# Joining score halves by an accumulating DMA in one slot of four, instead of on VectorE in one slot of five

## The chip, the core and the metric

The kernel runs on one core of a Trainium2 chip. The metric is the device time of one execution in microseconds. A core has five engines that run their own instruction queues: TensorE (PE, matrix products), VectorE (DVE), ScalarE (ACT), GpSimd (POOL) and SyncE (SP, which here only issues DMAs). They wait for each other through semaphores.

## The reference

The program is a stack of four graph layers on x of shape (64, 256, 128) with one 256 x 256 adjacency matrix. Layers 0 to 2 (a gated graph network of five steps, a Chebyshev layer and a plain graph convolution, each behind a layer norm and a relu, with a residual sum) make up, with the projections and outputs of layer 3, about a fifth of PE's busy time. The other four fifths are the scores of layer 3, an attention layer with a score for every pair of nodes:

```python
s1 = jnp.einsum('bkf,ef->bke', x, W1)
s2 = jnp.einsum('bkf,ef->bke', x, W2)
pre = s1[:, :, None, :] + s2[:, None, :, :] + b_lin
h = jnp.where(pre >= 0, pre, ALPHA * pre)
e = jnp.einsum('bije,e->bij', h, a) + bias
attn = jax.nn.softmax(e, axis=2)
out = jax.nn.sigmoid(jnp.einsum('bij,bjf->bif', attn, x))
```

For each of 64 batches and each of 256 x 256 pairs (i, j), 256 features e pass a leaky relu and are summed with weights a. The relu part is nonlinear in i and j together, so it has to be formed for every pair: 64 x 256 x 256 x 256 elements.

## The kernel before

Everything is float32. Two batches form a pair (NB = 2), so there are 32 pairs. The 256 features of a score are cut into two halves of 128, one feature to a partition: half 0 and half 1 (`k` in the code). The 256 rows i are cut into **slots**: a slot is four rows i, 32 apart, for both batches. A pair has 64 slots (two blocks `ic` of 32), the program 2048 (`NSLOT`).

A half of a slot is a tile `rl` of 128 partitions x (4 rows, 2 batches, 256 nodes j) = 128 x 2048 floats, 1 MiB. It holds min or relu terms of `s1[i] + s2[j]`, with the weights' sizes already folded into s1 and s2 (their signs are applied by the products on PE). PE then sums it over the features with four matmuls, side by side in four groups of 32 columns (`win` and `win_n` hold the signs and put the four rows at their place in the bank `pe`). Each float32 matmul shows as two records in the profile. There are 12 tiles `rl`.

A half-tile can be made by three engines:

- VectorE makes half 0 with one whole `tensor_tensor` of 128 x 2048 (L809).
- ACT makes half 1 with eight activations of 128 x 256 (L823).
- GpSimd makes either half with eight `tensor_scalar` of 128 x 256 (L835).

In one slot of five (`SHARE = (1, 5)`, 409 of 2048) the two halves are **joined** (`k == 2`): GpSimd makes a tile `z` of half 1 with a second form of row (L832, with the clamps `s1h` and `s1l`), and VectorE then adds half 0 into it with eight `scalar_tensor_tensor` (L801), which take the minimum and add what the tile holds. A joined tile goes to PE once instead of twice, so PE does 3687 half-tiles instead of 4096.

The order of each engine's instructions is fixed when the program is built. A small planner in the kernel keeps a clock for each engine (`clock`, advanced by `ran(engine, us, ...)` with durations written in the code), takes the engine whose time is least, and lets it do the first of what is ready: steps of a block's tail (softmax and output), then steps of a later pair's layers 0 to 2 (`front`), then score work. `in_order()` pins what was traced to that order. `part_of(e)` says which half an engine makes next, `tile_ready` when it could, `work_on_tile` does one part of it, `score` hands a finished tile to PE and returns it to `tiles` at the time when PE will have read it. `held` and `MOST` limit how many tiles each engine may have out. `partners` is the list of GpSimd's `z` tiles that wait for VectorE. The planned durations are, for example:

```python
done = ran(DVE, 1.55, since)      # four joining rows
done = ran(DVE, 2.2, since)       # a whole tile
done = ran(ACT, 1.43, since)      # four activations
done = ran(POOL, 1.06 if k == 2 else 0.9, since)   # two rows
```

Elsewhere in the pair's work GpSimd also does the subtraction of the gated step (L503), the inverse roots of the norms (L329, L330), a product of the norm (L402) and additions in the tail (L687, L725, L726), and VectorE waits for some of these.

Of the kernel before, what the change touches and what calls it, by code (L numbers as in the profile page):

```python
# [10 lines left out]
OP = mybir.AluOpType  # L11
# [4 lines left out]
NB = 2  # L16
# [4 lines left out]
MOST_NEGATIVE = -3.4028234663852886e38  # L21
PE, DVE, ACT, POOL = ENGINES = (mybir.EngineType.PE, mybir.EngineType.DVE, mybir.EngineType.Activation, mybir.EngineType.Pool)
SLOTS = 64
SHARE = (1, 5)
AHEAD_OF = 2


@with_exitstack
def kernel(
# [50 lines left out]
    nc = tc.nc  # L80
# [22 lines left out]
    def ran(engine, us, *after):  # L103
        start = max(clock[engine], 0.0, *after)
        if engine == ACT:
            behind[0] = max(0.0, behind[0] - (start - clock[ACT])) + 0.024 * us
        clock[engine] = start + us
        return clock[engine] + SEEN[engine] + (behind[0] if engine == ACT else 0.0)
# [19 lines left out]
    last, done = {}, [0]  # L128
# [208 lines left out]
    def flat(t):  # L337
        return t.rearrange("p b n -> p (b n)")
# [393 lines left out]
    NSLOT = NPAIR * SLOTS  # L732
    tiles = [[relu_pool.tile([P, 4, NB, N], F32, name=f"rl{k}", bufs=1), 0.0] for k in range(12)]
    MOST = {DVE: 8, ACT: 3, POOL: 4}
    held = dict.fromkeys(MOST, 0)
    begun = {}
    made = []
    partners = []
    left = {}
    t_pe = {}  # L740
    t_s2v = [0.0, 0.0]
    TAILED = set()
    ALONE, JOINED = [], []
    for n in range(NSLOT):
        (JOINED if (n + 1) * SHARE[0] // SHARE[1] > n * SHARE[0] // SHARE[1] else ALONE).append(n)
    following = [0, 0, 0]

    def where(n):
        return n // SLOTS, n % SLOTS // 32, n % 32

    def slot(k):

        of = JOINED if k == 2 else ALONE
        return of[following[k]] if following[k] < len(of) else NSLOT

    def part_of(e):

        if e == DVE:
            return 0
        if e == ACT:  # L760
            return 1
        if slot(2) <= max(slot(0), slot(1)) + AHEAD_OF:
            return 2
        return 0 if slot(0) < slot(1) else 1

    def tile_ready(e):

        if e in begun:
            return 0.0
        if e == DVE and partners and min(partners)[1] <= slot(0) + AHEAD_OF:  # L770
            return min(partners)[0]
        k = part_of(e)
        n = slot(k)
        if n >= NSLOT or n // SLOTS not in READY or held[e] == MOST[e] or not tiles:
            return None
        since = READY[n // SLOTS]["since"]
        return max(since[k], min(t[1] for t in tiles))

    def work_on_tile(e):
        if e not in begun:  # L780
            if e == DVE and partners and min(partners)[1] <= slot(0) + AHEAD_OF:
                since, n, t = partners.pop(partners.index(min(partners)))
                held[POOL] -= 1
                begun[e] = [n, 2, t, since, 0]
            else:
                k = part_of(e)
                tiles.sort(key=lambda t: t[1])
                begun[e] = [slot(k), k, *tiles.pop(0), 0]
                following[k] += 1
            held[e] += 1  # L790
        n, k, t, free, part = begun[e]
        p, ic, r = where(n)
        ops = READY[p]
        i0 = ic * P + r
        if e == DVE and k == 2:
            since = max(ops["since"][0], free)
            parts = 2
            for g in (2 * part, 2 * part + 1):
                for b in range(NB):
                    i = i0 + g * 32  # L800
                    nc.vector.scalar_tensor_tensor(t[:, g, b, :], ops["s2a"][:, b, :], ops["s1"][0][:, b, i:i + 1], t[:, g, b, :],  # L801
                                                   op0=OP.min, op1=OP.add)
            done = ran(DVE, 1.55, since)
            t_s2v[p % 2] = max(t_s2v[p % 2], done)
        elif e == DVE:
            since = max(ops["since"][k], free)
            whole = [P, 4, NB, N]
            rows = ops["s1"][0][:, :, i0:i0 + 97:32].rearrange("p b g -> p g b").unsqueeze(3)
            nc.vector.tensor_tensor(t, rows.to_broadcast(whole), ops["s2a"].unsqueeze(1).to_broadcast(whole), op=OP.min)  # L809
            done = ran(DVE, 2.2, since)  # L810
            t_s2v[p % 2] = max(t_s2v[p % 2], done)
            parts = 1
        elif e == ACT:
            since = max(ops["since"][k], free)
            if "s2p" not in ops:
                ops["s2p"] = s2p
                nc.scalar.copy(s2p, ops["s2n"])
                ran(ACT, COPY, since)
            parts = 2
            for g in (2 * part, 2 * part + 1):  # L820
                for b in range(NB):
                    i = i0 + g * 32
                    nc.scalar.activation(t[:, g, b, :], s2p[:, b, :], AF.Relu, bias=ops["s1"][1][:, b, i:i + 1], scale=-1.0)  # L823
            done = ran(ACT, 1.43, since)
        else:
            since = max(ops["since"][k], free)
            parts = 4
            for b in range(NB):
                i = i0 + part * 32
                row = slice(i, i + 1)  # L830
                if k == 2:
                    nc.gpsimd.tensor_scalar(t[:, part, b, :], ops["s2z"][:, b, :], ops["s1h"][:, b, row], ops["s1l"][:, b, row],  # L832
                                            op0=OP.min, op1=OP.max)
                else:
                    nc.gpsimd.tensor_scalar(t[:, part, b, :], ops["s2n" if k else "s2c"][:, b, :], ops["s1"][k][:, b, row],  # L835
                                            MOST_NEGATIVE, op0=OP.min, op1=OP.max)
            done = ran(POOL, 1.06 if k == 2 else 0.9, since)
        begun[e][4] += 1
        if part + 1 == parts:
            del begun[e]  # L840
            if e == POOL and k == 2:
                partners.append((done, n, t))
            else:
                made.append((done, n, k, t, e))

    def score_ready():

# [15 lines left out]
    def score(tile_):  # L863
        since, n, k, t, e = tile_
        p, ic, r = where(n)
        block = p * NC + ic
        pe = pes[block % 2]
        first = block not in left
        if first:
            left[block] = 64  # L870
        made.remove(tile_)
        left[block] -= 2 if k == 2 else 1

        w = win[:, 1] if e == ACT else win_n[:, k % 2]
        for g in range(4):
            nc.tensor.matmul(pe[g * 32:(g + 1) * 32, :], w[:, 31 - r:63 - r], flat(t[:, g]),  # L876
                             start=first, stop=(left[block] == 0), skip_group_check=True)
        free = ran(PE, PROJECT, since, t_pe.get(block - 2, 0.0))
        tiles.append([t, free])
        held[e] -= 1  # L880
        scored[0] += 2 if k == 2 else 1
        if left[block] == 0:
            begin((p, ic), tail(p, ic, pe, free, READY[p]["x3"], READY[p]["h3"]))
# [42 lines left out]
    while scored[0] < 2 * NSLOT or CHAINS:  # L926
        while begun_fronts[0] < NPAIR and begun_fronts[0] < 2 + (scored[0] + 2 * SLOTS - 1) // (2 * SLOTS):
            begin_front()
        e = min(now, key=now.get)
        todo = []  # L930
        for key in CHAINS:
            since = chain_ready(key, e)
            if since is not None:
                todo.append((since, (0, key) if isinstance(key, tuple) else (1, key), key))
        if e == PE:
            best = score_ready()
            if best:
                todo.append((best[0], (2,), best[1]))
        else:
            since = tile_ready(e)  # L940
            if since is not None:
                todo.append((since, (2,), None))
        ready = [x for x in todo if x[0] <= now[e] + 0.05]
        if ready:
            _, (rank, *_), what = min(ready, key=lambda x: x[1])
            if rank < 2:
                advance(what)
            elif e == PE:
                score(what)
            else:  # L950
                work_on_tile(e)
            in_order()
            now[e] = max(now[e], clock[e])
        else:
            later = [x[0] for x in todo] + [t for t in now.values() if t > now[e]]
            now[e] = min(later) if later else now[e] + 1.0
# [31 lines left out]
```

## Time and profile before

| | us |
|---|---|
| median of 3 runs | 5054.16 (5053.93 to 5054.52) |
| the profiled execution | 5031.67 |
| its span, first to last instruction | 5029.9 |
| idle of VectorE in the span | 199.3 |
| idle of ACT in the span | 230.8 |
| idle of GpSimd in the span | 195.7 |

Granted TensorE clock over the span: 0.996. The first 120 us are a ramp: the constants are prepared and the first pair goes through layers 0 to 2 before scores can start; GpSimd is busy 15.8 us of these 120. DMA is idle most of the time: 37.38 MB are moved in the whole span, 7 GB/s.

How to read it: busy time counts instructions as the profiler saw them, per engine and not counting DMA issues, branches or semaphore waits. A group's row gives the line and engine, what it writes and reads, the count, the busy time, the mean duration of one instruction in ns, and the idle time of the engine just before them with what ended it. Neighbouring instructions of one engine overlap, so a mean times a count can exceed the busy time. A row of the waits reads: who waited, for whom, microseconds in total, times, and the longest.

### The profile page before, as it was taken

How to read it: one execution, taken by the hardware profiler on the slowest of the kernel's cores; microseconds unless marked ns; L12 is line 12 of the kernel's file. 1: busy time of each engine (PE TensorE's matmuls, PEld its weight loads, DVE VectorE, ACT ScalarE, POOL GpSimd, SP SyncE). 2: the span in 40 equal slices, each digit the busy share in tenths (PEclk: the TensorE clock that was granted, in tenths of full speed). 3: DMA queues.
4: the chain of work that ended last, by engine and by line, in shares of the span. 5: the costliest groups of instructions: out<-in, count | busy, mean ns of one | idle time of the engine just before them, and what ended most of it. 6: DMA issues, size and time to landing. Idle time of an engine off the chain costs nothing.

```text
span 5029.9 us, 137362 instructions
## 1 busy us (share of the span) xinstructions
PE 4926.6 (98%) x52817; PEld 1791.9 (36%) x52817; DVE 4830.6 (96%) x6767; ACT 4799.1 (95%) x12553; POOL 4834.2 (96%) x9670
## 2 busy tenths in 40 slices
PE   7999999999999999999999999999999999999999
PEld 3333333333333333333333333333333333333332
DVE  3999999999999999999999999999999999999998
ACT  3999999999999999999999999999999999999999
POOL 1999999999999999999999999999999999999998
PEclk9999999999999999999999999999999999999999
DMA  0000000000000000000000000000000000000000
GB/s 20 8 7 6 9 5 9 9 5 8 7 7 9 6 7 8 8 6 8 6 8 8 6 9 6 8 8 5 9 8 5 9 8 6 8 5 6 6 5 4
DMA packets 60356, 37.38 MB, mean 7 GB/s; under 512 B 4528, under 2 KB 59696, under 8 KB 59696
## 3 DMA queue, kind: packets, MB, share of 16 engines
q1 hardware_dynamic: 58976, 28.59, 2.4%
q8 instruction: 413, 6.77, 0.6%
q14 instruction: 247, 2.02, 0.1%
q10 hardware_dynamic: 720, 0.00, 0.0%
HBM read 18.09 MB, written 10.49 MB: 6 GB/s over the span
## 4 chain that ended last, share of the span: by engine, by line
PE 43%; POOL 25%; DVE 23%; ACT 7%; issue 3%; DMA 0%; POOLq 0%; ACTq 0%; DVEq 0%
PE bank L876 26%; PE bank L335 14%; POOL rl L835 13%; DVE rl L809 12%; POOL rl L832 9%; ACT rl L823 6%; DVE rl L801 5%; POOL d L503 1%; PE bank L363 1%; DVE hT L510 1%; DVE bank L506 1%; DVE stats L395 1%; POOL mv L330 1%; PE bank L356 1%; POOL sc L687 0%
## 5 line engine op out<-in xcount | busy, mean ns | idle before, releaser
L823 ACT ACTIVATE rl<-bank,s1b 128x256 f32<-128x256 f32 x10536 | 4186.4, 908 | 9.2 <-PE bank L876 7.3
L809 DVE TENSOR_TENSOR rl<-s1a,bank 128x2048 f32<-128x2048 f32 x1269 | 2841.4, 2274 | 1.3 <-PE bank L876 1.2
L876 PE MATMUL bank<-rl,win_n 128*32 128x512 f32 x18960 | 2458.7, 595 | 26.7 <-DVE rl L809 19.4
L832 POOL TENSOR_SCALAR rl<-s2z,s1h,s1l 128x256 f32<-128x256 f32 x3272 | 1750.5, 551 | 0.0
L876 PE MATMUL bank<-rl,win 128*32 128x512 f32 x10536 | 1436.5, 594 | 0.0
L835 POOL TENSOR_SCALAR rl<-s2c,s1a 128x256 f32<-128x256 f32 x2960 | 1339.3, 474 | 14.0 <-ACT s1a L667 2.1
L801 DVE SCALAR_TENSOR_TENSOR rl<-bank,s1a,rl 128x256 f32<-128x256 f32 x3272 | 1324.7, 471 | 1.7
L835 POOL TENSOR_SCALAR rl<-s2n,s1b 128x256 f32<-128x256 f32 x2576 | 1167.7, 475 | 9.0
L876 PEld LDWEIGHTS bank<-rl,win_n 128*32 128x32 f32 x18960 | 629.5, 110 | 1339.8 <-issue 949.6
L876 PEld LDWEIGHTS bank<-rl,win 128*32 128x32 f32 x10536 | 356.1, 110 | 697.0 <-issue 567.0
L335 PE MATMUL bank<-mT,wts 128*32 128x512 f32 x2560 | 344.0, 593 | 1.2 <-DVE rh L468 1.2
L335 PE MATMUL bank<-adj_t,h 128*32 128x256 f32 x5120 | 315.3, 383 | 4.0 <-ACT h L522 3.8
L503 POOL TENSOR_TENSOR d<-d,hT 128x512 f32<-128x512 f32 x155 | 199.2, 1285 | 54.3 <-ACT d L499 54.3
L335 PEld LDWEIGHTS bank<-adj_t,h 128*32 128x32 f32 x5120 | 169.2, 111 | 166.2 <-issue 53.6
L406 ACT ACTIVATE h<-x,mv 128x128 f32<-128x128 f32 x384 | 168.2, 590 | 50.5 <-POOL mv L402 50.1
L412 ACT COPY mT<-bank 128x512 f32<-128x512 f32 x160 | 144.9, 906 | 42.9 <-PE bank L335 31.1
L506 DVE SCALAR_TENSOR_TENSOR bank<-bank,d 128x512 f32<-128x512 f32 x160 | 110.6, 692 | 72.2 <-POOL d L503 71.5
L464 ACT ACTIVATE bank<-bank,gate_b 128x512 f32<-128x512 f32 x160 | 160.2, 1001 | 16.9 <-PE bank L335 15.8
L335 PE MATMUL bank<-hT,wts 128*32 128x512 f32 x1280 | 175.2, 593 | 0.0
L335 PE MATMUL bank<-mT,w 128*32 128x512 f32 x1280 | 169.9, 593 | 0.0
L335 PE MATMUL bank<-rh,u5t 128*32 128x512 f32 x1280 | 169.8, 592 | 0.0
L487 ACT ACTIVATE bank<-bank,gate_b 128x512 f32<-128x512 f32 x160 | 153.6, 960 | 15.1 <-PE bank L335 15.0
(134 smaller groups left out, 3507.9 us busy)
## 6 DMA issues: line engine op xcount, KB each, us to landing
xin<-in_x_dram SPq DMA_DIRECT2D x64, 128.0 KB, 2.3
lin<-row SPq DMA_DIRECT2D x32, 256.0 KB, 7.7
out_dram<-o SPq DMA_DIRECT2D x64, 128.0 KB, 1.8
row<-quarter SPq DMA_DIRECT2D x32, 64.0 KB, 1.5
w_raw<-in_L_gnn_w_w_dram SPq DMA_DIRECT2D x3, 128.0 KB, 3.0
th_raw<-in_L_gnn_Theta_dram SPq DMA_DIRECT2D x1, 320.0 KB, 3.9
adj_n<-in_adj_dram SPq DMA_DIRECT2D x1, 256.0 KB, 3.2
w_raw<-in_L_gnn_u_w_dram SPq DMA_DIRECT2D x2, 64.0 KB, 2.9
```

The lines of the kernel that those rows point to most:

```text
L335: nc.tensor.matmul(o[g:g + 32], w[:, g:g + 32], t, start=start, stop=stop, skip_group_check=True)
L406: nc.scalar.activation(h[:, k, :], s[:, k, :], AF.Relu, bias=mv[:, k, 0:1], scale=mv[:, k, 1:2])
L464: nc.scalar.activation(r[0], pr[0], AF.Tanh, bias=br, scale=0.5)
L487: nc.scalar.activation(pr[0], pr[0], AF.Tanh, bias=bz, scale=0.5)
L503: nc.gpsimd.tensor_sub(d, d, hT)
L506: nc.vector.scalar_tensor_tensor(by_feature(pr[0]), by_feature(pr[0]), 1.0, d, op0=OP.add, op1=OP.mult)
L801: nc.vector.scalar_tensor_tensor(t[:, g, b, :], ops["s2a"][:, b, :], ops["s1"][0][:, b, i:i + 1], t[:, g, b, :], op0=OP.min, op1=OP.add)
L809: nc.vector.tensor_tensor(t, rows.to_broadcast(whole), ops["s2a"].unsqueeze(1).to_broadcast(whole), op=OP.min)
L823: nc.scalar.activation(t[:, g, b, :], s2p[:, b, :], AF.Relu, bias=ops["s1"][1][:, b, i:i + 1], scale=-1.0)
L832: nc.gpsimd.tensor_scalar(t[:, part, b, :], ops["s2z"][:, b, :], ops["s1h"][:, b, row], ops["s1l"][:, b, row], op0=OP.min, op1=OP.max)
L835: nc.gpsimd.tensor_scalar(t[:, part, b, :], ops["s2n" if k else "s2c"][:, b, :], ops["s1"][k][:, b, row], MOST_NEGATIVE, op0=OP.min, op1=O ...
L876: nc.tensor.matmul(pe[g * 32:(g + 1) * 32, :], w[:, 31 - r:63 - r], flat(t[:, g]), start=first, stop=(left[block] == 0), skip_group_check= ...
```

## The change

In a joined slot both halves are now made as ordinary tiles: half 0 by VectorE or GpSimd in their ordinary way, half 1 by GpSimd in the `z` form. When both are done, GpSimd issues one DMA that reads `z` and adds it into half 0's tile; PE takes the sum. The joining rows on VectorE are gone. The share goes from one slot in five to one in four (512 slots). In the planner, half 0's sequence now runs over all slots, half 1's over those that aren't joined, and `z` over the joined ones; an issue is planned at 0.7 us of GpSimd (`ISSUE`), a sum at 4.0 us of the DMA queue (`ADDED`) and 3.0 us more until it has landed (`LANDED`), and the issue is offered 0.3 us after the pair is done (`SLACK`), only between GpSimd's tiles. `z` is free when the sum has landed.

```diff
-SHARE = (1, 5)
+SHARE = (1, 4)
 AHEAD_OF = 2
+ISSUE, ADDED, LANDED, SLACK = 0.7, 4.0, 3.0, 0.3
...
-    partners = []
...
-    ALONE, JOINED = [], []
-    for n in range(NSLOT):
-        (JOINED if (n + 1) * SHARE[0] // SHARE[1] > n * SHARE[0] // SHARE[1] else ALONE).append(n)
+    JOINED = [n for n in range(NSLOT) if (n + 1) * SHARE[0] // SHARE[1] > n * SHARE[0] // SHARE[1]]
+    WITH = set(JOINED)
+    ORDER = [range(NSLOT), [n for n in range(NSLOT) if n not in WITH], JOINED]
     following = [0, 0, 0]
+    pairs = {}
+    adding = [0.0]
...
-        if e == DVE and k == 2:
-            since = max(ops["since"][0], free)
-            parts = 2
-            for g in (2 * part, 2 * part + 1):
-                for b in range(NB):
-                    i = i0 + g * 32
-                    nc.vector.scalar_tensor_tensor(t[:, g, b, :], ops["s2a"][:, b, :], ops["s1"][0][:, b, i:i + 1], t[:, g, b, :],
-                                                   op0=OP.min, op1=OP.add)
-            done = ran(DVE, 1.55, since)
-            t_s2v[p % 2] = max(t_s2v[p % 2], done)
-        elif e == DVE:
+        if e == DVE:
...
-            if e == POOL and k == 2:
-                partners.append((done, n, t))
+            if n in WITH:
+                pairs.setdefault(n, {})[k] = done, t, e
             else:
                 made.append((done, n, k, t, e))
+
+    def pair_ready():
+
+        return min(((max(x[0] for x in both.values()), n) for n, both in pairs.items() if len(both) == 2), default=None)
+
+    def add_pair(n):
+        (since, t, e), (since_z, z, e_z) = pairs[n][0], pairs.pop(n)[2]
+        nc.gpsimd.dma_start(out=t.rearrange("p g b n -> p (g b n)"), in_=z.rearrange("p g b n -> p (g b n)"), accum_op=OP.add)
+        issued = ran(POOL, ISSUE, since, since_z)
+        adding[0] = max(adding[0], issued) + ADDED
+        done = adding[0] + LANDED
+        held[e] -= 1
+        held[e_z] -= 1
+        tiles.append([z, done])
+        made.append((done, n, 2, t, None))
...
             if since is not None:
-                todo.append((since, (2,), None))
+                todo.append((since, (3,), None))
+            pair = pair_ready()
+            if e == POOL and pair and e not in begun:
+                todo.append((pair[0] + SLACK, (2,), pair[1]))
...
+            elif rank == 2:
+                add_pair(what)
             else:
                 work_on_tile(e)
```

## Prediction

> **What bounds the kernel now.** I read the busy table first, then the costliest groups, then the waits of GpSimd and VectorE, last the busy time by stretch and a piece of the timeline.
>
> ```profile
> span 5029.9 us, 137362 instructions
> PE 4926.6 (98%) x52817; PEld 1791.9 (36%) x52817; DVE 4830.6 (96%) x6767; ACT 4799.1 (95%) x12553; POOL 4834.2 (96%) x9670
> ```
>
> Four engines are full at once, so a gain has to lighten all four, or lighten the tightest by no more than its lead over the next. PE's figure is modelled at its ends: in the timeline the matmuls of consecutive half-tiles begin 0.86 us apart (2513.04, 2513.90, 2514.76), while a half-tile counts 1.06 us busy (3895.2 us of L876 over 3687 halves). So some 0.2 x 3687 = 740 us of PE's busy time on this line is overlap, and PE has slack that its 98% hides. PE follows; it doesn't lead.
>
> ```profile
> L823 ACT ACTIVATE rl<-bank,s1b 128x256 f32<-128x256 f32 x10536 | 4186.4, 908 | 9.2 <-PE bank L876 7.3
> L809 DVE TENSOR_TENSOR rl<-s1a,bank 128x2048 f32<-128x2048 f32 x1269 | 2841.4, 2274 | 1.3 <-PE bank L876 1.2
> L832 POOL TENSOR_SCALAR rl<-s2z,s1h,s1l 128x256 f32<-128x256 f32 x3272 | 1750.5, 551 | 0.0
> L835 POOL TENSOR_SCALAR rl<-s2c,s1a 128x256 f32<-128x256 f32 x2960 | 1339.3, 474 | 14.0 <-ACT s1a L667 2.1
> L801 DVE SCALAR_TENSOR_TENSOR rl<-bank,s1a,rl 128x256 f32<-128x256 f32 x3272 | 1324.7, 471 | 1.7
> L835 POOL TENSOR_SCALAR rl<-s2n,s1b 128x256 f32<-128x256 f32 x2576 | 1167.7, 475 | 9.0
> ```
>
> The producers of score halves are here, with almost no idle before them. Instructions of one engine overlap, so I divide busy time by count: ACT row 0.397 us, DVE whole tile 2.239, DVE joining row 0.405, GpSimd z row 0.535, GpSimd plain row 0.453 (2507.0 / 5536). Which engine is tightest shows in who waits:
>
> ```profile
> POOL d L503 <- ACT d L499: 54.3, 4, 16.1
> POOL mv L329 <- DVE mv L397: 34.8, 6, 17.0
> ...
> DVE bank L506 <- POOL d L503: 71.5, 62, 6.5
> ...
> DVE nmx L691 <- POOL sc L687: 15.3, 20, 2.1
> DVE x L598 <- POOL rn L330: 13.8, 16, 2.1
> ```
>
> GpSimd's two long waits fall into the ramp (10 waits, up to 17 us). From 200 to 4900 us it waits 1.0 us in all, while VectorE waits 83.3 us there on GpSimd (the last three rows, cut to that stretch: 55.6, 15.3 and 12.4). GpSimd is busy 4633 of those 4700 us, the rest being gaps between its own instructions; VectorE 4594, ACT 4555. **GpSimd leads**, by 39 us over VectorE and 78 over ACT. What the change puts on GpSimd decides.
>
> **What the Trainium skill says.** (1) "DMA: Bandwidth & Descriptors", section "Latency and other measured facts": a DMA issued by GpSimd takes about 1 us to its first byte, the time of the Q7 cores that write descriptors. The trace before has no DMA of GpSimd; SyncE's issue slices in the timeline are 0.34 and 0.36 us. (2) Same page, "Anatomy of one DMA — SWDGE (gpsimd) path": about 2.0 us plus bytes over 436 GB/s. "Collectives: The Full Stack", section "The bandwidth ceiling: the fold count and why AG ≠ RS ≠ AR", says that an add in the DMA reads two sources. No run here shows either; the largest transfer in the trace is 256 KB. (3) "SBUF — State Buffer", section "Who interferes with whom": DMAs don't contend with compute engines, and a VectorE instruction with one SBUF input doesn't contend with GpSimd. The trace agrees as far as it goes: the plain GpSimd rows have median 473 and minimum 458 ns, with VectorE at 96% beside them.
>
> **The change, part by part.** Counts come from the instruction orders of both kernels; each busy time is count by the durations above.
>
> VectorE loses 3272 joining rows (1324.7 us) and gains 571 whole tiles (1840 instead of 1269): 571 x 2.239 = 1278.5. Net -46 us.
>
> ACT loses 112 rows: 112 x 0.397 = -44 us.
>
> PE loses 412 matmuls, that is 103 of 3687 halves: 103 x 0.86 = -89 us. 409 joined slots become 512.
>
> GpSimd gains 824 z rows (4096 instead of 3272): +440.8. It loses 2008 plain rows (3528 instead of 5536): 2008 x 0.453 = -909.4. Net -468.6 before the 512 DMAs it now issues. **So an issue may cost 468.6 / 512 = 0.915 us before GpSimd is as loaded as today.**
>
> The issue is the unknown. Below: SyncE's 0.34 us, where GpSimd's own instruction would only start it. Above: 1.0 us by the skill's first-byte price, and up to 2.0 if two source reads double the descriptors. Nothing excludes values over 1.0. I take 0.7, the middle of 0.34 and 1.0; it is also what the kernel's own plan reserves (ISSUE), whose other GpSimd entries agree with the trace (0.9 for two plain rows against 0.906, 1.06 for two z rows against 1.07). GpSimd then stands at -468.6 + 358.4 = -110 us.
>
> The wait that the issue adds: GpSimd must see VectorE's half (and its own z) done, and its queue stands still behind it. In the new order at least one further GpSimd tile (8 rows, 3.6 to 4.3 us) lies between z's last row and the issue in 504 of 512 cases, and today GpSimd waits on VectorE 1 us in the steady stretch; I cost this at nothing, at worst some 0.1 us a time, 50 us, which the 110 us cover.
>
> The transfer: one tile is 1 MiB. Estimate from the page: 2.0 + 2 x 1.049 MB / 436 GB/s = 6.8 us; the plan allows 4.0 queued plus 3.0. One sum is due every 4970 / 512 = 9.7 us, so the DMA queue keeps up unless a sum takes over 9.7. SyncE's queue is untouched. Latency costs buffers, not time: holding times (making, some 2 us of waiting, 0.9 on PE; z 17 us and its partner 18 us, with 6 us of waiting and 7 of landing) add up to about 7 of the 12 tiles (36 ms of holding over 4970 us). Five spare tiles let a sum land about 5 x 4970 / 1024 = 24 us later than planned. PE's new wait for the sums I therefore cost at nothing.
>
> The sum: with GpSimd 110 us lighter, what is late next is VectorE or ACT. VectorE: 4784.4 busy and today's 199.3 us of idle is 4984; a third of the 83 us it waits on GpSimd may go, giving 4956. ACT: 4754.6 + 230.8 = 4985 with all its idle kept. I take a span of 4970, 60 us less. The profiled execution took 5031.67 us, 22.5 less than the median of the runs, 5054.16; I carry that over: 5054 - 60 = **4994 us**, -1.2%. (A measurement of this kernel tells about 0.2%, 10 us, from no change.)
>
> **The rivals.**
>
> *The issue becomes GpSimd's bound (slower).* One mechanism: the Q7 cores write descriptors for one target and two sources, and GpSimd's next row waits for them. It decides from 0.915 us; each 0.1 above adds 51 us, as GpSimd has no idle to give. At 1.0: 5054 + 44 = 5098; at 1.1: 5149; at 2.0: 5610. For it: the page's 1 us and GpSimd's lead. Against: first-byte time is latency[...]. From 0.80 down VectorE binds instead, and a cheaper issue gains nothing more.
>
> *The DMA is too slow (slower).* If an add in the DMA takes 12 us of the queue, 512 x 12 = 6144 us of span. Against it: 2.4 us of bytes per MiB, twice, leaves nearly half of the 9.7.
>
> *Gain eaten (same).* An issue of 0.9 to 0.93, or 0.8 plus 0.1 of waiting for VectorE's half each time: about 5054.
>
> *Not as said?* The order holds 512 DMAs and no joining row, so it does what it says; only the times are open.
>
> **How the numbers follow.** Issue under 0.89 and sums on time: 0.57. Level, 0.09. Issue above: 0.28. DMA late or rate-bound: 0.06. Likeliest: 4994, with its own range 4950 (all of VectorE's 83 us gone: 4784 + 116 = 4900, half believed) to 5040. To hold 8 in 10 it has to reach into the slower case up to an issue of 1.1: 5150. Left out: dearer issues and a slow DMA, some 0.15, and 0.03 below. Faster 0.57, same 0.09, slower 0.34.
>
> **What would show it.** In the profile after: no joining row on VectorE, 1840 whole tiles near 2.24 us; 512 issues on GpSimd's queue. Right: GpSimd's busy time near 4366 us (issues aren't counted), gaps of about 0.7 us around issues, VectorE's waits on GpSimd shorter, PE's waits on the DMA a few tens of us. Wrong by the first rival: gaps of 0.9 us or more at issues, VectorE's and PE's waits on GpSimd rows grown, GpSimd again without waits. Wrong by the second: PE or the rows that reuse a tile waiting on the DMA by hundreds of us.

## The result, and the profile after

The changed kernel took 5028.64 us (median of 4) against 5054.33 us before (4): ratio 0.9951, interval 0.9934 to 0.9968, a gain of 0.5%. Measured again beside other runs it took 5014.61 us (6 executions, 5005.26 to 5026.62) against 5029.99 (28): ratio 0.997 (0.9958 to 0.9981). Executions of the kernel before fall on two levels, near 5030 and near 5054, and no trace shows why. So below a variant is set against the changed kernel as it ran beside the same figure of before: 5028.6 where before has its median at 5054, and 5014.6 where it has it at 5030 (the runs again, with eleven tiles, and with both plan entries). Differences of 20 us across the two are not read.

The first table of the page after, to set beside that of before:

```profile
span 5030.7 us, 133280 instructions
PE 4827.5 (96%) x51993; PEld 1741.7 (35%) x51993; DVE 4806.1 (96%) x4066; ACT 4768.8 (95%) x12441; POOL 4754.5 (95%) x8998
```

Every engine has less to do: PE -99 us, VectorE -25, ACT -30, GpSimd -80. The profiled executions have the same span (5029.9 before), but they don't compare the kernels: that of before is 22 us faster than the other executions beside it, that of the changed kernel isn't. All four engines idle more: PE 203 us instead of 103, VectorE 225 instead of 199, ACT 262 instead of 231, GpSimd 276 instead of 196.

The costliest groups (busy us, mean ns; then idle time before the group's instructions, and what ended most of it); first PE's score line as it was before, then the page after:

```profile
L876 PE MATMUL bank<-rl,win_n 128*32 128x512 f32 x18960 | 2458.7, 595 | 26.7 <-DVE rl L809 19.4
...
L807 ACT ACTIVATE rl<-bank,s1b 128x256 f32<-128x256 f32 x10424 | 4147.6, 772 | 72.4 <-PE bank L875 54.0
L793 DVE TENSOR_TENSOR rl<-s1a,bank 128x2048 f32<-128x2048 f32 x1840 | 4098.0, 2277 | 90.2 <-DMA rl<-rl 43.6
L875 PE MATMUL bank<-rl,win_n 128*32 128x512 f32 x18248 | 2296.1, 597 | 108.9 <-DVE rl L793 70.6
L816 POOL TENSOR_SCALAR rl<-s2z,s1h,s1l 128x256 f32<-128x256 f32 x4096 | 2224.6, 620 | 16.7 <-PE bank L875 9.5
L819 POOL TENSOR_SCALAR rl<-s2n,s1b 128x256 f32<-128x256 f32 x1864 | 858.2, 517 | 23.9 <-PE bank L875 10.8
L819 POOL TENSOR_SCALAR rl<-s2c,s1a 128x256 f32<-128x256 f32 x1664 | 764.3, 516 | 12.8 <-DMA rl<-rl 0.4
L836 POOL DMA_DIRECT2D rl<-rl x512 | 414.3, 811 | 23.8 <-DVE rl L793 12.2
```

The counts are those of the orders: no joining row, 1840 whole tiles, 512 issues. What is new stands right of the second bar. VectorE's whole tiles had 1.3 us of idle before them; now 90.2. ACT's rows had 9.2; now 72.4. PE's `win_n` matmuls had 26.7; now 108.9. The issue is 414.3 / 512 = 0.81 us busy; unlike what stands above on how to read the page, GpSimd's busy time counts these issues.

The waits of VectorE, ACT and PE after (total us, times, longest):

```profile
DVE rl L793 <- DMA rl<-rl: 43.6, 30, 4.0
DVE rl L793 <- PE bank L875: 37.2, 45, 5.0
DVE bank L507 <- POOL d L504: 26.5, 23, 6.5
...
ACT rl L807 <- PE bank L875: 54.0, 41, 3.7
...
PE bank L875 <- DVE rl L793: 70.6, 75, 3.1
PE bank L364 <- DVE hT L511: 50.9, 52, 3.5
PE bank L875 <- DMA rl<-rl: 36.7, 30, 4.1
```

A row that makes a tile and waits for the DMA or for PE's score line waits for a **tile to come free**. Before, these waits on VectorE and ACT were 8.5 us; now they are 43.6 + 37.2 + 54.0 and 16.1 on ACT for the DMA: 151 us. VectorE's wait on GpSimd's L503 (71.5 before; L504 now) has shrunk to 26.5, as predicted.

The DMA queue of the sums and their landing, from the page after:

```profile
q0 software_dynamic: 73728, 536.90, 53.1%
...
rl<-rl POOLq DMA_DIRECT2D x512, 1024.0 KB, 7.5
```

The queue holds the engines for 0.531 x 5030.7 / 512 = 5.2 us a sum, where the plan says 4.0. A sum lands 7.5 us after its issue begins in the median (6.7 to 13.7); the plan says 0.7 + 4.0 + 3.0 = 7.7 for a sum that has the queue to itself. So a sum alone lands about when the order supposes. Those that queue behind another land later than supposed; in the trace 85 of the 512 issues start within 5.2 us of the one before.

### The profile page after: what moved, and what is told of

It reads as the page before. It is cut to its first block, busy times and chain, and to the rows that moved or that the text cites. A ratio compares the mean times of both kernels' runs of the same rounds, so it can differ in the third digit from the quotient of the medians.

```text
span 5030.7 us, 133280 instructions
## 1 busy us (share of the span) xinstructions
PE 4827.5 (96%) x51993; PEld 1741.7 (35%) x51993; DVE 4806.1 (96%) x4066; ACT 4768.8 (95%) x12441; POOL 4754.5 (95%) x8998
## 4 chain that ended last, share of the span: by engine, by line
PE 39%; DVE 27%; POOL 12%; DMA 7%; ACT 6%; issue 5%; POOLq 0%; DVEq 0%; ACTq 0%
PE bank L875 24%; DVE rl L793 21%; PE bank L336 13%; DMA rl<-rl 7%; POOL rl L816 5%; POOL rl L819 5%; ACT rl L807 4%; PE bank L364 1%; POOL rl L836 1%; DVE stats L396 1%; DVE hT L511 1%; DVE bank L507 1%; POOL d L504 1%; DVE rh L469 1%; PE bank L357 0%
## 5 line engine op out<-in xcount | busy, mean ns | idle before, releaser
L807 ACT ACTIVATE rl<-bank,s1b 128x256 f32<-128x256 f32 x10424 | 4147.6, 772 | 72.4 <-PE bank L875 54.0
L793 DVE TENSOR_TENSOR rl<-s1a,bank 128x2048 f32<-128x2048 f32 x1840 | 4098.0, 2277 | 90.2 <-DMA rl<-rl 43.6
L875 PE MATMUL bank<-rl,win_n 128*32 128x512 f32 x18248 | 2296.1, 597 | 108.9 <-DVE rl L793 70.6
L816 POOL TENSOR_SCALAR rl<-s2z,s1h,s1l 128x256 f32<-128x256 f32 x4096 | 2224.6, 620 | 16.7 <-PE bank L875 9.5
L875 PE MATMUL bank<-rl,win 128*32 128x512 f32 x10424 | 1382.0, 595 | 0.0
L819 POOL TENSOR_SCALAR rl<-s2n,s1b 128x256 f32<-128x256 f32 x1864 | 858.2, 517 | 23.9 <-PE bank L875 10.8
L819 POOL TENSOR_SCALAR rl<-s2c,s1a 128x256 f32<-128x256 f32 x1664 | 764.3, 516 | 12.8 <-DMA rl<-rl 0.4
L836 POOL DMA_DIRECT2D rl<-rl x512 | 414.3, 811 | 23.8 <-DVE rl L793 12.2
L504 POOL TENSOR_TENSOR d<-d,hT 128x512 f32<-128x512 f32 x155 | 214.1, 1381 | 60.5 <-ACT d L500 60.2
L465 ACT ACTIVATE bank<-bank,gate_b 128x512 f32<-128x512 f32 x160 | 147.9, 924 | 18.5 <-PE bank L336 17.4
L364 PE MATMUL bank<-ident,hT 128*128 128x128 f32 x640 | 105.6, 288 | 54.0 <-DVE hT L511 50.9
L336 PEld LDWEIGHTS bank<-mT,wts 128*32 128x32 f32 x2560 | 86.0, 111 | 192.5 <-issue 145.3
```

Source lines behind the costliest of these rows:

```text
L336: nc.tensor.matmul(o[g:g + 32], w[:, g:g + 32], t, start=start, stop=stop, skip_group_check=True)
L364: nc.tensor.transpose(pt[:, b, c, :], ht[:, b, c * P:(c + 1) * P], ident)
L465: nc.scalar.activation(r[0], pr[0], AF.Tanh, bias=br, scale=0.5)
L504: nc.gpsimd.tensor_sub(d, d, hT)
L836: nc.gpsimd.dma_start(out=t.rearrange("p g b n -> p (g b n)"), in_=z.rearrange("p g b n -> p (g b n)"), accum_op=OP.add)
```

## Experiments: what the sum costs

**No sums.** The order stays, the DMA goes; half 1 of the joined slots is left out of the scores.

```diff
-        nc.gpsimd.dma_start(out=t..., in_=z..., accum_op=OP.add)
```

> The changed kernel without the 512 sums: the plan and so the order of all other instructions is unchanged, but no DMA is issued and PE takes half 0's tile alone (half 1 of the joined slots is left out of the scores). Theory T (tiles: engines wait because z and its partner are held 7.5 us and more by a sum): all waits on the DMA and most on tile reuse go, and with them the issues' 414 us of GpSimd; time near 4960. Theory I (the issue on GpSimd costs the gain): the same near 4960, so this run gives only the sum of both. Theory P (PE and the dependences of layers 0 to 2 set the pace, VectorE's 25 us less is all there is): within 15 us of 5029.

4911.01 us, ratio 0.9729 (0.9705 to 0.9754), some 50 us below what the theories T and I expected. Theory P (the pace is set elsewhere) falls: against 5028.6 the sums cost the changed kernel 118 us in all. Its busy table:

```profile
PE 4784.2 (97%) x51993; PEld 1750.8 (36%) x51993; DVE 4775.6 (97%) x4066; ACT 4756.6 (97%) x12441; POOL 4396.2 (90%) x8486
```

Three engines are at 97%, GpSimd at 90% with room. The order is that of the changed kernel, so the difference of GpSimd's busy time is what the issues add to it: (4754.5 - 4396.2) / 512 = 0.70 us each. That is less than the 0.81 us of an issue's own record, because issues overlap the rows beside them.

**Short sums.** Each DMA carries 64 of 2048 columns; the other columns' sums are left out.

```diff
-...in_=z.rearrange("p g b n -> p (g b n)"), accum_op=OP.add)
+...in_=z.rearrange("p g b n -> p (g b n)")[:, 0:64], accum_op=OP.add)
```

(The destination is cut likewise.)

> The changed kernel with each sum cut to 64 of 2048 columns: the issue stays on GpSimd[...], the transfer shrinks to a thirty-second, order unchanged; the other columns' sums are left out. Theory T: as fast as the kernel without sums (near 4960), landing drops from 7.5 to about 2 us and the waits on the DMA (96 us on PE, VectorE, ACT) go. Theory I: as slow as the changed kernel, 5029, with an issue still near 0.81 us. Theory P: within 15 us of 5029 like the other.

4981.56 us (4969.56 to 4992.56), ratio 0.987 (0.9845 to 0.9895): between the theories. The executions form two groups, three near 4970 and three near 4992. The issue, the queue and the landing in its trace:

```profile
L836 POOL DMA_DIRECT2D rl<-rl x512 | 417.2, 817 | 15.1 <-DVE rl L793 8.6
...
q0 software_dynamic: 73728, 16.81, 4.1%
...
rl<-rl POOLq DMA_DIRECT2D x512, 32.0 KB, 2.2
```

The issue costs the same for 32 KB as for 1 MiB (0.815 and 0.809 us; the packets are as many, 144 a sum); landing falls from 7.5 to 2.2 us, and the waits on the DMA are gone (0.5 us left). So the **issue**, with what a short sum still takes, accounts for about 4982 - 4911 = 71 us, and the rest of the **transfer** for about 5029 - 4982 = 47 us. The two groups make each of these uncertain by 11 us.

## Experiments: the share

**VectorE's joining at one in four.**

```diff
-SHARE = (1, 5)
+SHARE = (1, 4)
```

(in the kernel before)

> The kernel before with its VectorE joining, but one slot in four joined: only the share moves. VectorE's joined slot costs 3.24 us against 2.24 for a half, GpSimd's z 4.28 against 3.62; PE has 103 halves less (-89 us). If the share alone brings PE's relief and PE sets the pace (P): up to 25 us faster than 5054. If VectorE and GpSimd set the pace: they get about 100 more joined slots, (103 x 1.0 us more on VectorE, 103 x 0.66 on GpSimd, 103 fewer halves of 3 to 4 us to make elsewhere): within 20 us of before, either way.

5124.45 us, ratio 1.0138 (1.0112 to 1.0164): my 20 us were wrong, it loses 71. By the expectation's prices the extra making is 103 x (1.0 + 0.66) = 171 us. Measured, the planner spreads somewhat more over three full engines: VectorE's busy time rises by 79 us (to 4909.8), ACT's by 83 (4881.7), GpSimd's by 67 (4901.3), while PE's 412 fewer matmuls buy nothing. Joining more slots is paid by the makers, not by one of them.

**The DMA's joining at one in five.**

```diff
-SHARE = (1, 4)
+SHARE = (1, 5)
```

(in the changed kernel)

> The changed kernel with one slot in five joined by a DMA (409 sums): the means of joining alone, at the share of before. 103 fewer issues and sums, 103 more halves on PE. T: fewer tiles held, fewer waits, but more making; between 5010 and 5035. P: PE back at 3687 halves, time 20 us or more over the changed kernel, near 5054.

5000.8 us (4989.16 to 5005.37), ratio 0.9905 (0.9884 to 0.9926): 28 us faster than one in four, and below the range of either theory. P falls again: PE had 103 halves more and the kernel was faster. The means of joining alone is worth more than the whole change; the larger share gave part of it back.

## Experiments: tiles and plan

**The changed kernel again.** No edit.

> The changed kernel again, unchanged, beside the others: executions of the kernel before fall on two levels, 5029.5 and 5053.7, and this tells on which levels the changed one falls. If the change brings the whole difference of the medians, 25 us, all its executions stay near 5028. If it has the same two levels, some come at about 5004.

5014.61 us, spread from 5005.26 to 5026.62: neither of the two cases expected.

**Eleven tiles** instead of twelve, in each kernel.

```diff
-... for k in range(12)]
+... for k in range(11)]
```

> The changed kernel with 11 tiles rl instead of 12 (the planner knows it and plans for it). Theory T (sums hold tiles and the 12 are too few): clearly slower, by 30 us or more over 5029, more waits of VectorE and ACT on PE's and the DMA's release of tiles. Theory P (pace set elsewhere, tiles to spare as the prediction said): within 10 us of 5029.

5093.82 us, ratio 1.0133 (1.0119 to 1.0146): 79 us lost.

> The kernel before with 11 tiles instead of 12. T: before, tiles are held shortly, so it loses little: within 10 us of 5054, less than a third of what the changed kernel loses by the same edit. P: the same loss in both.

5037.7 us, ratio 1.0015 (1.0008 to 1.0021): 8 us lost. The same edit costs the changed kernel ten times as much. GpSimd's largest wait in the changed kernel with 11 tiles:

```profile
POOL rl L816 <- DMA rl<-rl: 106.6, 22, 8.5
```

It waits for a tile that a sum still holds, 22 times and up to 8.5 us.

**Thirteen tiles**, with the ring of short-lived tiles cut from 12 to 9 buffers to make room.

```diff
-... for k in range(12)]
+... for k in range(13)]
...
-    SHORT = dict(tag="short", bufs=12)
+    SHORT = dict(tag="short", bufs=9)
```

> The changed kernel with 13 tiles rl; for their room the ring of short-lived tiles of layers 0 to 2 and the tails goes from 12 to 9 buffers, which may itself cost. With 11 tiles the changed kernel lost 79 us, the one before 8. If a tile more relieves the sums: 10 us or more under 5014. If the cut ring binds: above 5014, with new waits on layers 0 to 2, and it tells nothing on tiles.

5003.68 us, ratio 0.9899 (0.9887 to 0.9912): 25 us under 5028.6, with no run of the cut ring alone beside it. VectorE's waits for a tile fell from 80.8 to 18.1 us:

```profile
DVE rl L793 <- DMA rl<-rl: 10.8, 12, 2.8
DVE rl L793 <- PE bank L875: 7.3, 13, 1.4
...
PE bank L875 <- DMA rl<-rl: 33.5, 31, 3.8
```

PE's own wait for the sums stays (33.5 of 36.7). A tile more helps those who make tiles; it doesn't help PE, which is ordered to take some sums before they have landed. So tiles are a part, and the order is another.

**The plan's entries** raised: the queue's to what the trace shows, the issue's to 0.9, which lies above the 0.81 of its record and the 0.70 that it adds. Only the order of instructions and the division of halves change.

```diff
-ISSUE, ADDED, LANDED, SLACK = 0.7, 4.0, 3.0, 0.3
+ISSUE, ADDED, LANDED, SLACK = 0.9, 5.3, 3.0, 0.3
```

> The changed kernel with the plan's entries near what the trace shows (ISSUE 0.9 instead of 0.7: the issue is 0.81 us busy and about 0.1 us of gaps; ADDED 5.3 instead of 4.0: the queue is 53.1% busy, 5.2 us a sum; LANDED 3.0 kept). Only the order changes. If the misplanned order makes the waits on the DMA (96 us on PE, VectorE and ACT) they fall by half or more and the time drops to about 5005. If tiles are the cause, a later planned landing changes little: within 10 us of 5029.

4975.86 us (4973.78 to 4977.6), ratio 0.9892 (0.9879 to 0.9906) beside the 5029.99 of before: 39 us under the changed kernel in the same comparison, with the same 512 sums, the same issue (0.82 us) and the same landing (7.5 us). PE's waits in its trace:

```profile
PE bank L875 <- DVE rl L793: 89.0, 122, 3.1
PE bank L364 <- DVE hT L511: 29.4, 40, 2.4
PE bank L875 <- DMA rl<-rl: 6.7, 3, 5.0
```

Waits on the DMA are 6.7 us on PE, 1.4 on VectorE and 6.9 on ACT, 15 in all instead of 96, though the transfer is unchanged. What it still costs in this order isn't shown: no run has these entries with short sums. Which of the two entries did it:

```diff
+ISSUE, ADDED, LANDED, SLACK = 0.9, 4.0, 3.0, 0.3
```

> The changed kernel with only ISSUE planned at 0.9 us instead of 0.7 (ADDED stays 4.0): GpSimd gets fewer halves, the sums are still planned to land too early. Replanning both entries gave 4975.9 against 5014.6. If the late landing is the cause, this brings little: within 15 us of 5014. If GpSimd's overload by 0.11 us and more an issue (512 x 0.11 = 56 us) is the cause, this alone reaches 4985 or less.

4993.16 us (4987.0 to 4996.43), ratio 0.9877 (0.9864 to 0.989): 35 us under 5028.6, between the two cases expected. GpSimd makes 19 half-tiles fewer (152 rows), VectorE 10 and ACT 9 more. The waits on the DMA are only halved:

```profile
PE bank L875 <- DMA rl<-rl: 27.0, 24, 6.1
...
DVE bank L507 <- POOL d L504: 16.6, 6, 6.5
...
ACT h L407 <- POOL mv L403: 18.1, 20, 4.3
```

```diff
+ISSUE, ADDED, LANDED, SLACK = 0.7, 5.3, 3.0, 0.3
```

> The changed kernel with only ADDED planned at 5.3 us instead of 4.0 (ISSUE stays 0.7): sums are planned to land 1.3 us later, so PE and the reuse of tiles are ordered later. If the late landing is the cause: 4990 or less, and the waits on the DMA fall from 100 us to under 30. If GpSimd's overload is: within 15 us of 5014, the waits on the DMA fall all the same.

5022.15 us (5003.84 to 5026.48), ratio 0.9932 (0.9921 to 0.9943): 6 us under 5028.6. Its profiled execution, the fastest of the six, shows the waits on the DMA nearly gone (8.6 us on PE, 2.2 on VectorE, 6.9 on ACT). The waits on GpSimd are there instead, twice as long as with the issue's entry:

```profile
DVE bank L507 <- POOL d L504: 35.7, 23, 6.5
...
ACT h L407 <- POOL mv L403: 33.0, 32, 4.4
```

So most of the 39 us comes with the issue's entry, and waits on the DMA can go without the time following them. The two gains, 35 and 6, add up to about that of both; that one entry pays only with the other isn't shown. The likely reading is that with ISSUE at 0.7 the order gives GpSimd more than it does in time. Whether any other relief of GpSimd by some 19 half-tiles would do the same was not tried; the issue itself adds no more than the 0.7 that was planned.

**One in five with the new entries.**

```diff
-SHARE = (1, 4)
+SHARE = (1, 5)
...
+ISSUE, ADDED, LANDED, SLACK = 0.9, 5.3, 3.0, 0.3
```

> The changed kernel with both plan entries (0.9 and 5.3) and one slot in five joined (409 sums). With the old entries one in five was faster than one in four (5000.8). If that came only from the misplanned sums, one in four is now as fast or faster: here 4975 to 4995. If fewer sums are better in themselves: below 4970.

4977.7 us (4975.69 to 4980.53), ratio 0.9847 (0.9835 to 0.986): 23 us under one in five with the old entries. One in four with the new entries took 4975.86, but in the other comparison; so which share is better with them stays open. That the smaller share had won only because fewer of its sums were misplanned fits the expected range, and isn't shown. Both kernels beat the one before and the changed one.

## Why the prediction was right in direction and wrong in size

**Direction: right; mechanism: in part.** It is faster, by 26 us beside the figure of before that the forecast started from (15 in the second comparison), where 60 were forecast; the measured time lies inside the range of the likeliest case, 4950 to 5040. VectorE's and ACT's lighter load, GpSimd's shorter row list and VectorE's shorter waits on GpSimd are all in the trace. The next limit was not where the sum put it, at VectorE or ACT with the idle of today.

**The failed step: the waits costed at nothing.** "Latency costs buffers, not time", "about 7 of the 12 tiles", and "PE's new wait for the sums I therefore cost at nothing". Measured: waits for a tile on VectorE and ACT went from 8.5 to 151 us, PE waits 37 us for sums, and with the transfer cut to a thirty-second 47 us come back, more than the 34 that were missing. The occupancy was a mean, while sums can follow each other closely and then land up to 13.7 us after the issue; with one tile less the kernel loses 79 us, so there weren't five to spare. And the order is fixed at build time: it takes a sum from a queue that it advances by 4.0 instead of 5.2 us. I compared the queue's time with the 9.7 us between sums, which was right (the second rival didn't occur), but not with what the order supposes. The 6.8 us estimated for bytes and fixed cost against the planned 4.0 + 3.0 looked like agreement; they say nothing of how long a sum keeps the queue.

**The carried idle** is the same step seen in the sum. The floor of 4956 to 4985 kept the idle of VectorE and ACT, or took some off; in the profiles it grew by 25 and 31 us. Nor was it a floor: without the sums the kernel takes 4911, and VectorE and ACT idle 134 and 153 us there.

**The issue.** I took 0.7 us, and by the run without sums GpSimd's busy time grows by 0.70 an issue, under the 0.915 of the first rival. That rival did not occur: GpSimd waits more than before, it doesn't lead. But "a cheaper issue gains nothing more" was false: between short sums and none lie 71 us. And I read the plan's 0.7 as agreement, without asking what the order does with it; with 0.9 planned, 35 us come back. How 0.70 us on an engine that has room without them becomes that much isn't resolved.

**Two readings of the lines.** I added the busy times of groups that overlap each other. VectorE's whole tiles and joining rows are busy 4122 us together, not 2841.4 + 1324.7 = 4166, so its saving was 24 us and not 46. PE's two groups on the score line are busy 3447 us together, not 3895, so the slack hidden in its 98% is nearer 280 us than 740. The pitch of 0.86 us holds, though two of the three starts that I gave for it belong to L335. The largest transfer before was 320 KB, not 256.

**The offset.** The 22.5 us by which the median of before stood over its profiled execution is the distance between its two levels, 5030 and 5054. The changed kernel shows no such distance (profiled 5032.47, others 5028.3 to 5029.0). Carrying it did no harm only because before ran near 5054 again. It also makes the 10 us that I took for the least a measurement tells too fine.

**The prices used.** The 1 us of "DMA: Bandwidth & Descriptors", section "Latency and other measured facts", is a first-byte time and not how long GpSimd is held, which is 0.81 us here, and 0.70 net. The estimate from "Anatomy of one DMA — SWDGE (gpsimd) path" with the two sources of "Collectives: The Full Stack", section "The bandwidth ceiling: the fold count and why AG ≠ RS ≠ AR", 6.8 us, is close to the 7.5 us measured. Two sources fit the queue: 2 x 1.049 MB in 5.2 us are 403 GB/s of reading (a working from the trace; the reading itself isn't shown). The sentence on VectorE and GpSimd from "SBUF — State Buffer" holds there only outside VectorE's two-port modes, which the prediction left out. That DMAs don't slow the engines agrees with the traces: GpSimd's z rows have a median of 553 ns and VectorE's whole tiles one of 2277 or 2278 ns with the sums and without them.

**A rival not separated.** In the profiled execution of the changed kernel the granted TensorE clock dips more often than before (the figures are at the end). The mean is 0.992 instead of 0.996, at most some 20 us of PE's time; how much of it reaches the kernel's time was not tried.

## What to carry to other kernels

Where every engine is full and the order is fixed when the program is built, what an asynchronous step costs depends on what the plan supposes of it: here two planned durations were worth 39 us with the same transfers. Read issue, queue time and landing from the first trace, and try them in the plan before judging the step. A mean occupancy of buffers says little about spare ones; taking one buffer away, in both kernels, tells it in two runs. Groups of one engine overlap, so their busy times are not added: ask for the busy time of the instructions together. When a change carries two edits, such as the way of joining and its share, run each alone: here the way alone gained more than both.

## What the runs showed of the hardware

- The issue of an accumulating DMA on GpSimd is busy 0.81 us for 128 rows of 8 KB and 0.815 us for 128 rows of 256 bytes, with 144 packets a sum in both: at this number of rows it does not depend on the bytes. Landing does: 7.5 and 2.2 us.
- 512 such issues add 358 us to GpSimd's busy time in the same order, 0.70 us each.
- An accumulating DMA of 1 MiB from one tile to another holds the DMA engines for 5.2 us.
- Cut into slices of 25 us, the granted TensorE clock is below full in 15 slices after the first 200 us of the changed kernel, against 3 before; the mean falls from 0.996 to 0.992. PE waits more in the changed kernel; that the waits bring it about was not tried.
